# When a cross-attention batch stops counting as open, and the delay of the last two gate tiles

## The chip, the core and the metric

One core of one Trainium2 chip runs the whole program in one launch. The metric is device time in microseconds (us), from the start of an execution to its end. The core has five engines with a queue of their own: PE (TensorE, the matrix products), DVE (VectorE), ACT (ScalarE), POOL (GpSimd) and SP (SyncE, which here issues nearly all transfers). Each engine takes its queue in order, and waits at the head of the queue for what the next instruction needs.

## What is computed

A decoder of two layers over x of 4 batches, 512 rows and 512 columns, each sub-layer followed by a residual sum and a layer norm:

```python
x = ln(x + L0_attn(x))           # A: 4 heads of 128, rotary positions
x = ln(x + gamma*L0_xattn(x))    # B: 8 heads over ctx, softmax over the features
x = ln(x + L0_ffn(x))            # C: quantised gate and up (2048), Hadamard, down
x = ln(x + L1_attn(x))           # D: 16 heads of 32
x = ln(x + L1_xattn(x))          # E: one head over ctx, masked
x = ln(x + L1_ffn(x))            # F: 4-bit weights, 1408 wide, RMS norm

# E, per batch
scores = where(mask, x @ ctx.T / sqrt(512), -1e30)
out = softmax(scores) @ ctx      # zeros if the mask has no True

# C, per batch
h = silu(bitlinear(x, w_gate)) * bitlinear(x, w_up)
y = h_bitlinear(h, w_down)       # Hadamard over 2048, then the product
```

## The kernel before

Every sub-layer works on one batch at a time: 512 rows in four tiles of 128 rows. A unit of work is named by letter and batch, from A0 to F3 (24 of them, `ORDER`, line 38). Each unit is a Python generator. It emits some instructions, yields, and goes on at its next turn. A local `Pipe` (line 43) holds what is to be emitted some turns later: `pipe.later(n, ...)` files it, and each `pipe.tick()` counts one turn down. `pipe.drain()` makes turns with no new work until nothing is left.

**Who runs beside whom** is set by `lanes` (line 1254). One pass of its loop gives each open unit one turn, the older unit first, and then `step` gives one turn to background work. At most two units are open. The next of `ORDER` is opened when fewer than two are open, the same batch of the sub-layer before it is done, and the unit opened last has said "next" (`said >= times`). So a unit's place in the program follows from counting yields. The order of emission sets a priority and is not kept to the letter: the trace shows instructions that come long before their place where their inputs and buffers are free.

**Background work** is listed in `BESIDE` (line 40): a first unit, a last unit, and a key. The key "F" is `l1_ffn_weights`, 33 turns in which the weights of F are brought in: for each of 11 groups two loads of `gu` and one of packed codes `p`, which five turns later are unpacked by DVE and split by ACT and POOL (`p4h`, `p4l`). It gets a turn in each pass while the unit opened last is E2. What is still missing is fetched by `need` inside F0.

**Sub-layer E** (`l1_xattn`, from line 1015), counted in turns from its opening at 0: at 0 the loads of x and of the four ctx_t tiles (`ecT`); at 2 to 5 the four transposes of x (`ex`, split into a high and a low part by ACT and DVE); at 7 the loads of the four ctx tiles (`ecn`), and at 7 to 10 the scores (`es`, twelve products a row tile); "next" at 8; from 10 to 13 minimum and exponent (`ee`, DVE then ACT); at 14 to 17 the transposes `ep`; at 19 to 22 the value products (`pv`, twelve a row tile, in `value_rows`, line 419, which A uses too); at 20 to 23 the residual sums; at 24 the root of the layer norm (`finish`, line 229), at 26 the four norms (line 235, DVE) and at 27 the four stores of x (line 238, SP). At 28 it ends.

**Sub-layer C** (`l0_ffn`, line 607): from turn 9 on, sixteen gate tiles o = 0 to 15, one a turn. Tile o goes through five stages: the products `pg` and `pu` on PE; `gate` (DVE product, ACT Silu), one turn later; `up` (DVE product, ACT copy to `hh`, POOL difference to `hl`), two turns later; `had` (two products on PE), two turns later; `keep` (ACT copy to `hw`), one turn later; and the store to `had_scratch`, two turns later. Then the pipe is drained, sixteen loads bring the scratch back as `z`, two turns pass, and the second Hadamard product (`had2`, line 755) begins.

**Buffers**: pool `o` has 69 tiles of 512 floats a partition (ctx pairs, transposed pairs, F's weights), `t` 13, `x` 12 (three batches), `w` 4 (packed codes before they are split), all on line 27. Eight PSUM banks are shared by all products.

Of the kernel before, what the change touches and what calls it, by code (L numbers as in the profile page):

```python
# [21 lines left out]
B, S, D = 4, 512, 512  # L22
P = 128
NT = 4
# [12 lines left out]
F_SCALED, F_ACT, F_PAIR, F_DOWN = 1, 5, 3, 9  # L37
ORDER = "A0 A1 A2 A3 B0 B1 B2 B3 C0 C1 C2 C3 D0 D1 D2 D3 E0 E1 E2 E3 F0 F1 F2 F3"

BESIDE = [("A1", "A3", "C0"), ("A3", "B0", ("B", 0)), ("B0", "B2", "C"), ("C3", "D0", "D"), ("D1", "D3", "F0"), ("E2", "E2", "F")]  # L40


class Pipe:
# [25 lines left out]
class Net:  # L69
# [349 lines left out]
    def value_rows(self, pipe, pT, v, x, r, phase, b):  # L419

        nc = self.nc
        ln = self.ln_tile()

        def add(ps, i):
            nc.vector.scalar_tensor_tensor(x[i], ps, r[:, i : i + 1], x[i], ALU.mult, ALU.add)
            self.ln_stats(x[i], i, ln)

        for i in range(NT):
            pipe.tick()
            ps = self.pa("pv")  # L430
            self.mm3(ps, [(self.cols(pT[j], slice(i * P, (i + 1) * P)), v[j]) for j in range(NT)])
            pipe.later(1, add, ps, i)
            yield
        yield from pipe.drain()
        self.finish(pipe, x, ln, phase, b)
        yield from pipe.drain()
# [170 lines left out]
    def l0_ffn(self, b):  # L607
        nc = self.nc
        pipe = Pipe()
# [41 lines left out]
            yield  # L651
        scratch = self.had_scratch[b % 2]

        def gate(o, pg, pu):
            g = self.t("g")
            nc.vector.tensor_tensor(g, pg, arow, ALU.mult)
            nc.scalar.activation(g, g, AF.Silu)
            pipe.later(2, up, o, pu, g)

        def up(o, pu, g):  # L660
            nc.vector.tensor_tensor(g, pu, g, ALU.mult)
            hi, lo = self.t("hh", F32R), self.t("hl", F32R)
            nc.scalar.copy(hi, g)  # L663
            nc.gpsimd.tensor_tensor(lo, g, hi.bitcast(F32), ALU.subtract)  # L664
            pipe.later(2, had, o, hi, lo)

        def had(o, hi, lo):
            ph = self.pb("ph")
            nc.tensor.matmul(ph, self.had, hi, start=True, stop=False)
            nc.tensor.matmul(ph, self.had, lo, start=False, stop=True)  # L670
            pipe.later(1, keep, o, ph)

        def keep(o, ph):
            w = self.t("hw")
            nc.scalar.copy(w, ph)

            to = scratch[:, o * P : (o + 1) * P, :].rearrange("i p t -> p i t")
            pipe.later(2, lambda: nc.sync.dma_start(to, w.rearrange("p (i t) -> p i t", i=NT)))

        tern = self.tern  # L680
        for o in range(16):
            pipe.tick()
            c, m = o // 4, slice((o % 4) * P, (o % 4) * P + P)
            self.need("C", lambda: (3, c) in tern["wu_t"])
            pg, pu = self.pa("pg"), self.pa("pu")
            for k in range(NT):
                nc.tensor.matmul(pg, tern["wg_t"][k, c][:, m], qT[k], start=k == 0, stop=k == NT - 1)  # L687
            for k in range(NT):
                nc.tensor.matmul(pu, tern["wu_t"][k, c][:, m], qT[k], start=k == 0, stop=k == NT - 1)  # L689
            pipe.later(1, gate, o, pg, pu)  # L690
            yield "next" if o == 6 else None
# [562 lines left out]
def lanes(order, task, step):  # L1254

    todo = [(e.strip("+!"), e[0] == "+", max(1, e.count("!"))) for e in order]
    plain = [name for name, _, _ in todo]
    live, done = {}, set()  # L1260
    n, said = 0, 9
    while todo or live:
        if todo and len(live) < 2:
            name, soon, times = todo[0]
            before = chr(ord(name[0]) - 1) + name[1]
            if (before in done or before not in plain) and (said >= times or not live or soon):
                todo.pop(0)
                live[name] = task(name)
                last = name
                n, said = n + 1, 0  # L1270
        for name, g in list(live.items()):
            word = next(g, "end")
            if word == "end":
                live.pop(name)
                done.add(name)
            elif word == "next" and name == last:
                said += 1
        step(n)


def body(tc, args, phases=range(6)):
    with ExitStack() as ctx:
        net = Net(ctx, tc, args)
        net.gamma = net.load(net.c("gamma", [P, 1]), args["gamma"].to_broadcast([P, 1]))
        if 0 in phases:
            net.l0_attn_weights()
        net.bg = {("B", 0): net.l0_xattn_ctx(0), "C0": net.l0_ffn_scales(), "C": net.l0_ffn_weights(), "D": net.l1_attn_weights(), "F0": net.l1_ffn_codes(), "F": net.l1_ffn_weights()}
        f = [net.l0_attn, net.l0_xattn, net.l0_ffn, net.l1_attn, net.l1_xattn, net.l1_ffn]
        plain = ORDER.replace("+", "").replace("!", "").split()
        order = ORDER.split() if len(phases) == 6 else ["ABCDEF"[p] + str(b) for p in phases for b in range(B)]  # L1290

        def step(n):
            if len(phases) == 6:
                for first, last, key in BESIDE:
                    if plain.index(first) < n <= plain.index(last) + 1:
                        next(net.bg[key], None)

        def start(name):
            return f["ABCDEF".index(name[0])](int(name[1]))

        lanes(order, start, step)
# [68 lines left out]
```

## Time and profile before

| what | value |
|---|---|
| three runs, median (lowest to highest) | 1580.65 us (1579.52 to 1584.71) |
| the profiled execution's own time | 1581.65 us |
| its span, first to last instruction | 1580.0 us |
| granted TensorE clock, mean | 0.996 |
| PE busy | 1515.4 us, 96% |
| DVE busy | 1232.9 us, 78% |
| ACT busy | 1021.3 us, 65% |
| POOL busy | 666.2 us, 42% |
| C's gate products, first to last start | 461.6 to 691.0 us |
| E's loads of `ecn`, first to last issue | 1139.4 to 1249.9 us |

The profile is of one execution. A busy share is a mean over stages that differ; the time that PE spends idle, 64.6 us in all, is spread over the program in short waits. A row of a timeline gives the start, the duration, engine and line, the operation with the tile that it writes and those that it reads, and in brackets the idle time before it with what ended it. The stretch from about 1165 to 1262 us is E's.

### The profile page before, as it was taken

To read this page: it belongs to the slowest core of one execution; us is meant where nothing else is said; L and a number is where in the kernel's file an instruction comes from. 1 tells how busy PE (TensorE), PEld (TensorE's weight loads), DVE (VectorE), ACT (ScalarE), POOL (GpSimd) and SP (SyncE) were. 2 spreads that over 40 slices of the span, in tenths; PEclk is the share of its full clock that TensorE was granted. 3 is DMA by queue.
4 is the path that set the end of the run, shared out by engine and by line. 5 is a ranking of instruction groups with operands and counts; after the bars stand their busy time and mean duration, and the time that the engine had idled before them with its cause. 6 is when DMAs were issued, how large, how long until landed. Compare 5 with 4: busy or idle time off the path is not lost.

```text
span 1580.0 us, 25595 instructions
## 1 busy us (share of the span) xinstructions
PE 1515.4 (96%) x8222; PEld 1090.1 (69%) x8222; DVE 1232.9 (78%) x2658; ACT 1021.3 (65%) x2208; POOL 666.2 (42%) x672
## 2 busy tenths in 40 slices
PE   8999999999999999899999999999999999999996
PEld 6888786444544674477777668777687777777875
DVE  6486589999976688777577797767786888888896
ACT  5333336988878877888696864969634445545554
POOL 6673663555535303430435323353225344344342
PEclk9999999999999999999999999999999999999998
DMA  7043344455214744653434445633436630020101
GB/s 255 29 157 124 113 154 132 149 173 176 78 48 123 224 137 133 201 185 134 134 102 118 104 141 148 171 97 92 125 123 222 233 110 12 24 81 1 54 1 53
DMA packets 134150, 192.31 MB, mean 122 GB/s; under 512 B 17265, under 2 KB 52081, under 8 KB 134017
## 3 DMA queue, kind: packets, MB, share of 16 engines
q1 hardware_dynamic: 129888, 182.23, 36.3%
q0 software_dynamic: 4128, 8.46, 2.2%
q8 instruction: 65, 1.06, 0.3%
q14 instruction: 69, 0.56, 0.1%
HBM read 117.75 MB, written 47.71 MB: 105 GB/s over the span
## 4 chain that ended last, share of the span: by engine, by line
PE 63%; DVE 17%; ACT 8%; issue 6%; DMA 3%; POOL 3%; SPq 0%; ACTq 0%; DVEq 0%; POOLq 0%
PE fg L1185 7%; PE facc L1168 5%; PE dT L933 3%; DVE fg L1141 3%; PE pg L687 3%; PE had L755 2%; PE dn L741 2%; DVE bsm L474 2%; PE pu L689 2%; ACT de L923 2%; PE bo L498 2%; PE do L953 2%; PE qk L156 2%; PE qk L155 2%; PE qk L154 2%
## 5 line engine op out<-in xcount | busy, mean ns | idle before, releaser
L1141 DVE SCALAR_TENSOR_TENSOR fg<-fg,gs,fg 128x512 f32<-128x512 f32 x220 | 163.2, 745 | 30.9 <-ACT fg L1133 15.3
L923 ACT ACTIVATE de<-de,dm 128x128 f32<-128x128 f32 (+3 forms) x256 | 142.9, 563 | 11.3 <-DVE dm L919 10.9
L1185 PE MATMUL fg<-fxh,gu 128*128 128x512 f32 x352 | 140.2, 398 | 6.1 <-DVE fg L1141 3.1
L919 DVE CUSTOM_DVE_ANT_0 de<-ds,negm,thr 128x128 f32<-128x128 f32 (+3 forms) x256 | 126.4, 546 | 19.4 <-PE ds L908 16.0
L482 POOL TENSOR_SCALAR be<-be,bsm 128x512 f32<-128x512 f32 x128 | 96.5, 766 | 103.8 <-DVE bsm L480 72.7
L1185 PE MATMUL fg<-fxl,gu 128*128 128x512 f32 x352 | 137.4, 390 | 0.1
L664 POOL TENSOR_TENSOR hl<-g,hh 128x512 fp32r<-128x512 f32 x64 | 83.4, 1309 | 110.2 <-ACT hh L663 90.2
L1145 POOL TENSOR_TENSOR fg<-fg,fg 128x512 f32<-128x512 f32 x44 | 60.2, 1367 | 139.6 <-DVE fg L1141 60.0
L476 ACT ACTIVATE be<-bs,bsm 128x512 f32<-128x512 f32 x128 | 87.3, 690 | 31.1 <-DVE bsm L474 29.2
L845 POOL TENSOR_TENSOR dql<-dqf,dqh 128x512 fp32r<-128x512 f32 x32 | 41.4, 1295 | 150.8 <-ACT dqh L844 150.6
L933 PE MATMUL dT<-ident,de 128*128 128x128 f32 x640 | 92.0, 280 | 8.5 <-ACT de L923 6.4
L933 PEld LDWEIGHTS dT<-ident,de 128*128 128x128 f32 x640 | 72.3, 142 | 28.3 <-ACT de L923 14.0
L1185 PEld LDWEIGHTS fg<-fxh,gu 128*128 128x128 f32 x352 | 66.0, 188 | 30.1 <-DVE fg L1141 12.7
L474 DVE TENSOR_REDUCE bsm<-bs 128x1 f32<-128x512 f32 x128 | 83.4, 672 | 0.0
L498 PE MATMUL bo<-bpT,cT 128*64 128x512 f32 x256 | 76.7, 618 | 2.4 <-ACT bpT L489 1.2
L248 PEld LDWEIGHTS bT<-ident,be 128*128 128x128 f32 x512 | 54.9, 141 | 34.0 <-issue 11.5
L248 PE MATMUL bT<-ident,be 128*128 128x128 f32 x512 | 73.2, 281 | 3.6 <-POOL be L482 2.1
L1185 PEld LDWEIGHTS fg<-fxl,gu 128*128 128x128 f32 x352 | 66.1, 188 | 12.8 <-DVE fxl L146 0.4
L352 POOL TENSOR_TENSOR z<-z,rope_cos 128x512 f32<-128x512 f32 x32 | 46.8, 1473 | 64.8 <-DVE zs L349 57.8
L1133 ACT ACTIVATE fg<-fg,gs 128x512 f32<-128x512 f32 x88 | 60.1, 684 | 20.6 <-PE fg L1185 20.4
L687 PE MATMUL pg<-qT,tb 128*128 128x512 bf16 x256 | 66.8, 381 | 4.5 <-ACT qT L649 2.8
L1159 POOL TENSOR_TENSOR fhl<-fg,fhh 128x512 fp32r<-128x512 f32 x44 | 58.5, 1331 | 29.5 <-ACT fhh L1158 29.3
(355 smaller groups left out, 4640.3 us busy)
## 6 DMA issues: line engine op xcount, KB each, us to landing
x<-x SPq DMA_DIRECT2D x176, 256.0 KB, 3.0
had_scratch<-hw SPq DMA_DIRECT2D x64, 256.0 KB, 2.3
z<-had_scratch SPq DMA_DIRECT2D x64, 256.0 KB, 5.8
stk<-dqh SPq DMA_DIRECT2D x192, 64.0 KB, 2.1
tw<-in_wg_t SPq DMA_DIRECT2D x32, 256.0 KB, 3.8
tw<-in_wu_t SPq DMA_DIRECT2D x32, 256.0 KB, 3.7
tw<-in_wd_t SPq DMA_DIRECT2D x32, 256.0 KB, 2.8
p<-in_gu_p SPq DMA_DIRECT2D x22, 256.0 KB, 3.1
```

Source lines behind the costliest of these rows:

```text
L248: self.nc.tensor.transpose(pt[:, i * P : (i + 1) * P], srcs[i][:, j * P : (j + 1) * P], self.ident)
L474: nc.vector.tensor_reduce(sm[:, h : h + 1], ps, AX.X, ALU.max, negate=True)
L476: nc.scalar.activation(e, ps, AF.Exp, bias=sm[:, h : h + 1], accum_out=sm[:, 2 + h : 3 + h])
L482: nc.gpsimd.tensor_scalar(es[h][i], es[h][i], sm[:, 4 + h : 5 + h], 1.0, ALU.mult, ALU.mult)
L498: nc.tensor.matmul(po[0][h * 64 : h * 64 + 64, :], cT[j][:, c : c + 64], pTs[h], start=j == 0, stop=j == NT - 1)
L664: nc.gpsimd.tensor_tensor(lo, g, hi.bitcast(F32), ALU.subtract)
L687: nc.tensor.matmul(pg, tern["wg_t"][k, c][:, m], qT[k], start=k == 0, stop=k == NT - 1)
L919: nc.vector.tensor_tensor_reduce(es[i], ps, self.negm[:, 384 - P * i :], -1.0, self.thr[:, i : i + 1], ALU.add, ALU.min, n4[:, i : i + 1])
L923: nc.scalar.activation(es[i], es[i], AF.Exp, bias=n4[:, i : i + 1], scale=-1.0, accum_out=den[:, hh * 4 + i : hh * 4 + i + 1])
L933: nc.tensor.transpose(pt[:, o + (i - j) * P : o + (i - j + 1) * P], es[i][:, j * P : (j + 1) * P], self.ident)
L1141: self.emitted["DVE"] = nc.vector.scalar_tensor_tensor(y[u], ps, s, y[u], ALU.mult, ALU.add)
L1185: nc.tensor.matmul(ps, self.gu[i, u][:, g * P : (g + 1) * P], xT[g][n], start=n == 0, stop=n == 1)
```

## The change

Four edits. `value_rows` yields "tail" in place of nothing at its first value product if it runs for E. `lanes` notes such units and leaves them out when it counts how many are open; they still get their turns. The window of background work "F" begins with E1 in place of E2. And in C the delays between `gate` and `up`, `up` and `had`, `keep` and the store are one turn for the tiles 14 and 15 and two for the others.

```diff
-BESIDE = [..., ("D1", "D3", "F0"), ("E2", "E2", "F")]
+BESIDE = [..., ("D1", "D3", "F0"), ("E1", "E2", "F")]
...
             pipe.later(1, add, ps, i)
-            yield
+            yield "tail" if phase == 4 and i == 0 else None
...
+        lag = lambda o: 2 if o < 14 else 1
+
         def gate(o, pg, pu):
...
-            pipe.later(2, up, o, pu, g)
+            pipe.later(lag(o), up, o, pu, g)
...
-            pipe.later(2, had, o, hi, lo)
+            pipe.later(lag(o), had, o, hi, lo)
...
-            pipe.later(2, lambda: nc.sync.dma_start(to, w.rearrange("p (i t) -> p i t", i=NT)))
+            pipe.later(lag(o), lambda: nc.sync.dma_start(to, w.rearrange("p (i t) -> p i t", i=NT)))
...
-    live, done = {}, set()
+    live, done, tails = {}, set(), set()
...
-        if todo and len(live) < 2:
+        if todo and len(live.keys() - tails) < 2:
...
             elif word == "next" and name == last:
                 said += 1
+            elif word == "tail":
+                tails.add(name)
```

More of the change, by code (lines that the diff above doesn't have):

```diff
@@ L38 @@
 ORDER = "A0 A1 A2 A3 B0 B1 B2 B3 C0 C1 C2 C3 D0 D1 D2 D3 E0 E1 E2 E3 F0 F1 F2 F3"
-BESIDE = [("A1", "A3", "C0"), ("A3", "B0", ("B", 0)), ("B0", "B2", "C"), ("C3", "D0", "D"), ("D1", "D3", "F0"), ("E2", "E2", "F")]
+BESIDE = [("A1", "A3", "C0"), ("A3", "B0", ("B", 0)), ("B0", "B2", "C"), ("C3", "D0", "D"), ("D1", "D3", "F0"), ("E1", "E2", "F")]
 class Pipe:
```

## The prediction

> **What bounds the kernel now.** I read the page first.
>
> ```profile
> span 1580.0 us, 25595 instructions
> ## 1 busy us (share of the span) xinstructions
> PE 1515.4 (96%) x8222; PEld 1090.1 (69%) x8222; DVE 1232.9 (78%) x2658; ACT 1021.3 (65%) x2208; POOL 666.2 (42%) x672
> ```
>
> PE is busy in all but 1580.0 − 1515.4 = 64.6 us. The change takes no instruction away and adds none; it moves the places of instructions in the queues. So it can win only idle time of PE, and only in C and E and where they hand over. I therefore asked the table of windows for the stretches of E in which PE isn't full (first column the stretch, second its length, third PE's busy time).
>
> ```profile
> 1195.00:1200.00 5.00, 3.22 (x24) 2.27 (x22) 0.00 (x0) 4.85 (x11) 3.39 (x3) 1.00 0.98 332
> 1200.00:1205.00 5.00, 3.94 (x18) 2.82 (x19) 3.94 (x9) 4.67 (x11) 4.10 (x4) 1.00 1.05 397
> 1225.00:1230.00 5.00, 4.74 (x26) 3.40 (x24) 4.97 (x11) 3.42 (x8) 1.76 (x2) 1.00 0.17 49
> 1240.00:1245.00 5.00, 4.41 (x18) 3.04 (x18) 4.22 (x11) 3.27 (x9) 2.81 (x4) 1.00 0.89 329
> 1250.00:1255.00 5.00, 3.94 (x28) 3.26 (x27) 1.72 (x6) 2.17 (x6) 1.27 (x1) 1.00 0.89 291
> 1255.00:1260.00 5.00, 3.96 (x20) 2.16 (x19) 2.73 (x7) 3.94 (x10) 0.00 (x0) 1.00 0.91 291
> ```
>
> Three holes: (a) 1195 to 1205, 1.78 + 1.06 = 2.84 us, where E1 hands over to E2; (b) 0.26 + 0.59 = 0.85 us before and in E3's first scores; (c) 1250 to 1260, 1.06 + 1.04 = 2.10 us, where E3's scores are done and F0 begins. Together 5.79 us; the rest of 1165 to 1262 has next to none. Then the waits of ACT and of SP in E say why (total, times, longest).
>
> ```profile
> ACT ecnh L143 <- DMA ecn<-in_ctx: 15.9, 4, 8.0
> SPq L238 <- DVE x L235: 54.9, 9, 25.8
> SPq L252 <- POOL p4l L146: 19.5, 4, 8.8
> ```
>
> ACT's queue holds the copies `ecnh` ahead of the exponents `ee`. The copies wait for `ecn`. Those loads stand on SP behind the stores of the batch before, and the stores wait for the norms. Last, the timeline of DVE, POOL and PE around (c).
>
> ```profile
> 1189.31 1.92 DVE L235 TENSOR_SCALAR x<-x,ln 128x512 f32<-128x512 f32 x4
> 1244.64 4.85 DVE L235 TENSOR_SCALAR x<-x,ln 128x512 f32<-128x512 f32 x4
> 1244.79 4.42 POOL L146 TENSOR_TENSOR ecnl<-ecn,ecnh 128x512 fp32r<-128x512 f32 x3 [2.17 <-DMA ecn<-in_ctx]
> 1254.21 0.33 PE L248 MATMUL ep<-ident,ee 128*128 128x128 f32 x1 [1.06 <-ACT ee L1042]
> 1256.82 0.50 PE L1185 MATMUL fg<-fxh,gu 128*128 128x512 f32 x1 [0.65 <-DVE fxl L146]
> ```
>
> Four norms take 1.92 us, or 4.85 us when POOL's differences run beside them.
>
> **The "tail" edit.** I counted the yields of every unit. Before, E1 opens 22 passes after E0, E2 9 after E1, E3 20 after E2, F0 9 after E3. After it, 20, 9, 11 and 9. E1 to E2 stays at 9, since there it is "next" (turn 8) that decides. So E shrinks by 11 passes, but a pass has no length of its own; what counts is which PE work lies beside which wait.
>
> Hole (c): before, E3's drain has only F0's four transposes beside it. After, E2's value products stand at E3's turns 8 to 11: tiles 0 and 1 between E3's scores, tile 2 with the last of these, tile 3 behind it. 48 value products ran from 1170.67 to 1181.68, so a row tile costs 11.0/4 = 2.75 us. Tile 3 alone covers more than the 2.10 us. E1's stores also get ready long before E3's scores end, because these are spread over 8 × 2.75 = 22 us in place of 11. What is late next is `fxl`: E2's four sums, statistics and aggregates (0.74 + 0.69 + 0.17 = 1.60 each, 6.4 us) and norms stand among them on DVE. I take 2.0 of 2.1; ends 0 and 2.1.
>
> Hole (b): E3's transposes come when E2 is in its drain and E1 still has value products, so its first scores don't follow bare on E2's last product. I take 0.85; ends 0 and 0.85.
>
> Hole (a): E1 and E2 stand to each other as before, so nothing new covers the wait for the last exponent. Only E1's loads come two passes earlier against E0's stores. Of E1's four `ecn` loads two went at 1180.63, two after the stores at 1191.76. If all go first, ACT is free when the scores end; the chain minimum 0.68, exponent 0.72 + 0.18 remains, about 1.6 us behind the last product, E2's transposes cover part of it, and the second half, E2's split, shrinks likewise. I take half, 1.4; ends −2.9 and +2.8 (the lower end is that hole once more). E in sum: 2.0 + 0.85 + 1.4 = 4.25 us.
>
> **The window edit.** Its passes are 20 before (E2 open to E3 open) and 20 after (9 + 11), so as much of F's weights is brought in: fourteen `gu` and six `p` loads, five groups unpacked. Each unpack costs DVE about 1.7 us (0.54 + 0.48 + 0.68), ACT 0.62, POOL 1.29. All lie beside PE work. What moves are the places on SP: the loads now stand among E1's, not E2's, and a `p` load waits for `p4l` to free a buffer of pool `w`, up to 8.8 us. I cost it at nothing, because in (a) it is E0's stores that come last; uncovered it is the second rival.
>
> **The delay edit.** Per batch the drain loses two turns (tile 13 is now last: 8 turns after the last product become 6), so C2 opens 2 passes earlier and D0 4. From `had` of the last tile to `had2` there are six turns before and after, so the wait for `z` (1.33 us at 557.71, 0.40 at 709.40) stays. PE in the passes of the four drains: full in 500 to 520, 538 to 553 and 682 to 698; 16.32 of 18 us in 646 to 664. Only there is something to win, since `had2` of C2 joins C3's gate products two passes sooner. I take 0.7 of 1.7. On the other side, the chain gate to `had` takes 0.68 + 0.63 + 0.69 + 0.62 + 1.28 = 3.9 us, and PE's cover falls from five passes to three, 2.2 us each where gate products run alone: 6.6 us. Three POOL differences (3.8 us) now meet in two passes. If the cover fails, PE waits one such difference a batch: 4 × 1.28 = 5.1 us. Ends −5.1 and +1.7.
>
> **Sum.** 4.25 + 0.7 = 4.95 us off the profiled execution's 1581.65 (1580.0 of span, 1.65 around it): 1576.7. That execution lies 1.0 us above the median of the runs, 1580.65, so the forecast for the median is 1575.7.
>
> **A rule against it.** The norm rows above show 2.93 us more beside POOL. The Trainium skill, "SBUF — State Buffer", section "Who interferes with whom", says that VectorE in a two-port mode and GpSimd exclude each other from a shared pair of ports, and that the later one blocks fully. Three open batches mean more such meetings: by the rule each of E0 to E2 would pay up to that row's 2.93 us. By it the sum would lose up to 8.8 us if stores were still ahead of the loads that matter; by the row it loses nothing in (c), where the stores now come early.
>
> **The rivals.**
> 1. Order by readiness: the queues follow inputs and buffers more than passes. For it: E3's x was loaded at 1193, when E3 opens near 1233; F's first codes were unpacked by DVE at 1158.9, 40 us ahead of their place. Against it: PE's products keep the order of the passes through all of E. Then about a fifth of the gain comes, 1579.7.
> 2. Slower, by buffers and SP. At E2's last scores the count of `o` tiles by place is 25 for E2 (ctx pairs 8, x pairs 8, second ctx pairs 8, one `ee`), 16 for E1, 24 for F's weights (14 + 10): 65 of 69. Before it was 25 + 16 + 12 = 53. So loads can run ahead less, and the `p` waits come in front of E1's or E2's ctx loads. Price: the longest wait, 8.8 us, in front of `ecn` of E1, whose last pair went only 2.7 us ahead of the end of its scores; the 1.4 us of (a) is lost too. 1575.7 + 1.4 + 8.8 = 1585.9. It decides once such waits pass 4.95 + 4.7 = 9.7 us against the forecast. Against it: DMA is idle in 1185 to 1190 (share 0.04).
> 3. The shortened delay leaves PE waiting for `hl`: 1575.7 + 0.7 + 5.1 = 1581.5. Against it: ACT, not POOL, is nearly full there.
> 4. Much more: every hole of E closes (5.8), C's passes give 1.7, and the start of F0, where PE idles 3.0 us in 1280 to 1325 behind DVE, gains by work done earlier: 10.5 to 12 us, 1569 to 1570.
>
> **Numbers.** 0.3%, 4.7 us, is about what a measurement of this kernel can tell from no change. The bounds are 1575.9 and 1585.4. Forecast 0.52, its own range 1572 to 1577.5 (faster 0.45, same 0.07); rival 1 0.12 (same); rival 2 0.24 (slower 0.21, same 0.03); rival 3 0.06 (same); rival 4 0.06 (faster). Faster 0.51, same 0.28, slower 0.21. The range takes in all but the outer parts of 2 and 4: 1569 to 1587.
>
> **What would show it.** Right: PE full in the last scores of E3, with `pv` among them; all four `ecn` of E1 ahead of E0's stores; `z` waits as before; PE idle lower by some 5 us, all of it in E. Wrong: SP waiting for `p4l` in front of ctx loads; PE waiting for `hl` near `had`; new holes in D or F. The forecast falls if the holes only move to F0's start, where DVE is full.

## The result, and the profile after

The changed kernel takes 1589.97 us (median of 6 runs, 1587.99 to 1591.86); the kernel before took 1583.15 us beside it (1579.52 to 1584.71). The ratio is 1.0043, 95% interval 1.0032 to 1.0055: slower by some 6.8 us. The forecast was 1575.7 us, and the time lies above its range (1569 to 1587). The profiled execution that is read below took 1590.53 us, 1588.7 of it span.

The page of the changed kernel, its head (busy time of each engine, with its share of the span):

```profile
span 1588.7 us, 25593 instructions
PE 1516.9 (95%) x8222; PEld 1093.2 (69%) x8222; DVE 1229.9 (77%) x2658; ACT 1020.0 (64%) x2208; POOL 664.7 (42%) x672
```

The work is the same. TensorE's idle time went from 64.6 us to 1588.7 − 1516.9 = 71.8 us. To see where, I cut both profiled executions at the first matmul of C (`pg`), D (`dx`), E (`ex`) and F (`fg`):

| us | A and B | C | D | E | F |
|---|---|---|---|---|---|
| before | 461.6 | 284.3 | 395.3 | 115.6 | 323.2 |
| after | 462.1 | 288.4 | 395.0 | 118.9 | 324.3 |
| TensorE idle, before | 14.6 | 10.1 | 14.5 | 6.9 | 18.4 |
| TensorE idle, after | 15.4 | 12.9 | 14.6 | 9.5 | 19.4 |

The lengths are differences of starts rounded to a tenth. Each profile is of one execution, and a stage that an edit leaves alone varies as well: in the six profiles, here and below, with the old C and the old buffers, C takes 283.6 to 284.5 us; in the six with the old E and F, E takes 115.6 to 116.5 and F 323.1 to 324.0; A and B together, which no edit touches, take 460.0 to 463.9. So a microsecond in C, E or F says little, three or four do.

C got longer by 4.1 us and E by 3.3 us. E should have become shorter by 4.25. The windows of E around its largest hole (stretch, length, busy time of TensorE, its weight loads, VectorE, ScalarE, POOL, then the granted clock, DMA share and GB/s):

```profile
1195.00:1200.00 5.00, 5.00 (x29) 4.25 (x28) 0.00 (x0) 1.24 (x2) 1.54 (x2) 1.00 1.00 333
1200.00:1207.00 7.00, 0.61 (x6) 0.37 (x4) 4.96 (x8) 2.17 (x5) 4.31 (x4) 0.80 1.05 390
1207.00:1212.00 5.00, 4.39 (x17) 3.59 (x18) 3.33 (x7) 4.67 (x12) 3.98 (x4) 0.50 0.56 206
1212.00:1218.00 6.00, 4.90 (x21) 3.75 (x20) 5.93 (x10) 4.31 (x9) 4.20 (x3) 0.80 0.33 96
1218.00:1222.00 4.00, 4.00 (x19) 3.34 (x18) 2.05 (x4) 1.28 (x3) 0.66 (x1) 1.00 0.96 314
```

At 1200, hole (a)'s place in the order of work (E1's scores done, E2 next), TensorE stands still for 6.39 us (its row is below), and its granted clock is then 0.50 from 1207 to 1212. VectorE did nothing at all from 1195 to 1200. So the question is what VectorE stood before. Its timeline (start, duration, instruction, and in brackets how long it sat idle before it and what released it):

```profile
1192.66 1.92 DVE L235 TENSOR_SCALAR x<-x,ln 128x512 f32<-128x512 f32 x4
1201.97 1.22 DVE L1076 TENSOR_SCALAR p<-p,i 128x512 int32<-128x512 int32 x1 [7.38 <-DMA p<-in_dn_p]
1203.23 1.37 DVE L1077 TENSOR_SCALAR p<-p,i 128x512 int32<-128x512 int32 x1
1204.63 0.69 DVE L1103 SCALAR_TENSOR_TENSOR p<-p,p4s 128x512 f32<-128x512 f32 x1
1205.24 0.68 DVE L1043 CUSTOM_DVE_ANT_0 ee<-es,pen 128x512 f32<-128x512 f32 x1
```

After E0's norms the next entry of its queue is the unpacking of one of F's code groups (lines 1076, 1077, 1103), and that waits 7.38 us for its load. E1's minima (line 1043), for which ScalarE, TensorE and all of E wait, are queued behind it. TensorE's timeline shows the other end:

```profile
1206.83 0.47 PE L248 MATMUL ep<-ident,ee 128*128 128x128 f32 x1 [6.39 <-ACT ee L1044]
1215.58 0.49 PE L156 MATMUL es<-ecTh,exl 128*128 128x512 f32 x1 [1.10 <-DVE exl L146]
1269.17 0.50 PE L156 MATMUL pv<-ecnh,epl 128*128 128x512 f32 x1 [1.50 <-DVE epl L146]
```

The view names ScalarE's exponent as releaser, because that is the last link: minimum, exponent, transpose. The links before it tell the reason. ScalarE's timeline shows how much of the hole is the unpack's:

```profile
1198.50 1.28 ACT L143 CAST ecnh<-ecn 128x512 fp32r<-128x512 f32 x2 [4.30 <-DMA ecn<-in_ctx]
1200.14 0.62 ACT L143 CAST ecnh<-ecn 128x512 fp32r<-128x512 f32 x1 [0.37 <-DMA ecn<-in_ctx]
1200.67 0.61 ACT L143 CAST p4h<-p 128x512 fp32r<-128x512 f32 x1
1205.96 0.72 ACT L1044 ACTIVATE ee<-ee,em 128x512 f32<-128x512 f32 x1 [4.68 <-DVE em L1043]
```

Its copies of `ecn` wait for the context loads, as they did before the change, and end with one `p4h` at 1201.28. Only then does it wait for the minimum, for 4.68 us. So 4.68 of the 6.39 us are the unpack's. By these rows the other 1.7 us, an estimate, would be there without it, since the exponent is queued behind the copies.

And why was the code load late? The timelines of SP's queue and of POOL:

```profile
1193.24 1.78 SPq L238 DMA_DIRECT2D x<-x  x4
1195.08 1.78 SPq L252 DMA_DIRECT2D ecn<-in_ctx  x3
1197.43 0.38 SPq L252 DMA_DIRECT2D p<-in_dn_p  x1
```
```profile
1191.12 1.29 POOL L146 TENSOR_TENSOR p4l<-p,p4h 128x512 fp32r<-128x512 f32 x1 [0.67 <-ACT p4h L143]
```

The load goes out at 1197.43, behind E0's four stores, which wait for the norms, and three `ecn` loads. A `p4l`, which frees a buffer of pool `w`, had ended at 1192.41; the 5 us after that are SP's queue, and the 4.5 us from the issue to 1201.97 are the load itself. In the kernel before a like wait stood in another place: 2.77 us at 1209.84, under E2's scores, where TensorE had work.

```profile
1209.84 1.36 DVE L1074 TENSOR_SCALAR p<-p,i 128x512 int32<-128x512 int32 x1 [2.77 <-DMA p<-in_dn_p]
```

In C the largest new lines of TensorE's waits (total, times, longest) are, after:

```profile
PE ph L672 <- POOL hl L666: 3.1, 4, 1.0
PE had L757 <- DMA z<-had_scratch: 2.2, 2, 1.1
```

Before, the list of C's waits has none for `hl`, and that for `z` came to 1.7 us.

### The profile page after: what moved, and what is told of

Same layout as the page of the kernel before. It is cut to its first block, busy times and chain, and to the rows that moved or that the text cites. A ratio compares the mean times of both kernels' runs of the same rounds, so it can differ in the third digit from the quotient of the medians.

```text
span 1588.7 us, 25593 instructions
## 1 busy us (share of the span) xinstructions
PE 1516.9 (95%) x8222; PEld 1093.2 (69%) x8222; DVE 1229.9 (77%) x2658; ACT 1020.0 (64%) x2208; POOL 664.7 (42%) x672
## 4 chain that ended last, share of the span: by engine, by line
PE 61%; DVE 16%; ACT 9%; issue 6%; DMA 4%; POOL 3%; SPq 0%; ACTq 0%; DVEq 0%; POOLq 0%
PE fg L1187 7%; PE facc L1170 5%; PE dT L935 3%; DVE fg L1143 3%; PE dn L743 2%; PE bo L498 2%; PE pg L689 2%; PE do L955 2%; ACT de L925 2%; PE pu L691 2%; DVE bsm L474 2%; PE bT L248 2%; PE qk L156 2%; PE qk L155 2%; PE qk L154 2%
```

## The experiments

Theory W: the window edit makes E longer, since a code group's unpacking stands in VectorE's queue ahead of E1's minima and waits for its load. Rival R: E waits for the context loads, as rival 2 had it, and the code loads only stand beside that. For C: theory H (TensorE waits for `hl`) and theory O (the older batch's products now displace those of the younger). "Theory A" in the texts recorded ahead of the runs is theory W where a run is about E, and theory H where it is about `hl`.

### The parts by themselves

Four kernels on one chip. The first is the kernel before with the three `lag` lines alone; the second has the "tail" alone; the third has both "tail" and window, with `lag = lambda o: 2`; the fourth has the window alone:

```diff
-("E2", "E2", "F")]
+("E1", "E2", "F")]
```

> The kernel before with the delay edit alone. Theory A (two separate costs: in C the tensor engine waits for hl, in E the vector engine waits for packed codes): slower by 3 to 5 us, since D's first transposes start at 745.9 us before and 750.5 after the change; the waits of PE for hl at ph add up to about 3 us, against 0.3 before. Theory B (all of it comes from three open batches in E): within 1 us of before, and D starts at 746.

> The kernel before with the tail edit alone, background window still E2. Theory A: the unpacking of F's codes no longer stands ahead of E1's minima, so the hole of 6.4 us is gone and the gain forecast for E shows: faster by 2 to 5 us, unless F0 then misses weights (the window has 11 passes in place of 20), which would cost some of it. Theory B: three open batches crowd the buffers and SP: slower by 3 us or more, with holes before E2 and E3.

> Tail and window edits without the delay edit. Theory A: the 6.4 us hole before E1's ep transposes is there, some of the gain at E3 and F0 too: slower by 2 to 4 us, and together with the delay edit alone this sums to the whole change (6.8 us). Theory B: slower by all of 6.8 us.

> The kernel before with the window edit alone: two open batches as before, F's weights from E1 on. Theory A: E1's drain meets the unpacking as in the changed kernel (the same passes after E1 opens), so a hole of about 6 us before E1's ep transposes and no gain at E3: slower by 3 to 6 us. Theory B: no third batch, so within 1 us of before.

The median of before on that chip was 1580.54.

| kernel | median | ratio [95%] | C | E | F |
|---|---|---|---|---|---|
| delay alone | 1583.04 | 1.0017 [1.0009, 1.0026] | 286.9 | 115.6 | 323.1 |
| tail alone | 1579.56 | 0.9996 [0.9987, 1.0005] | 283.8 | 111.4 | 326.6 |
| tail and window | 1585.53 | 1.0032 [1.0020, 1.0045] | 284.5 | 119.1 | 323.7 |
| window alone | 1587.45 | 1.0046 [1.0033, 1.0060] | 283.6 | 123.7 | 320.2 |

Three things follow. The parts add up: 2.5 us for the delay and 5.0 for tail and window make 7.5, where the whole change has 6.8. The window by itself, with two open batches as before, costs 6.9 us: E +8.1, F −3.0. So theory B, that three open batches are the cost, falls. And the tail by itself makes E 4.2 us shorter, but F 3.4 us longer, and the time is the same within what can be told. The delay cost less than expected (2.5 us for 3 to 5), the window more (6.9 for 3 to 6; with the tail 5.0 for 2 to 4).

The 4.2 and 3.4 us are not all idle time. E is cut at F's first `fg`, and with the tail more of E3's products come after that cut: TensorE is busy 1.8 us less in E and 1.0 us more in F. Its idle time falls by 2.5 us in E (6.9 to 4.4) and grows by 2.4 us in F (18.4 to 20.8). TensorE's longest waits around E with the tail alone:

```profile
1195.64 0.33 PE L248 MATMUL ep<-ident,ee 128*128 128x128 f32 x1 [0.95 <-ACT ee L1044]
1199.58 0.50 PE L154 MATMUL es<-ecTh,exh 128*128 128x512 f32 x1 [1.54 <-DVE exl L146]
1255.87 0.50 PE L156 MATMUL pv<-ecnh,epl 128*128 128x512 f32 x1 [1.51 <-DVE epl L146]
```

(b) and (c) are gone, which is the 2.5 us. (a) stays with all its size (0.95 and 1.54 us; the two waits were 1.01 and 1.33 before), and a wait for `epl` is new. What F lost is seen in the windows 1275 to 1325, for the kernel before:

```profile
1275.00:1325.00 50.00, 46.98 (x198) 36.16 (x197) 47.37 (x74) 27.06 (x45) 27.58 (x21) 1.00 0.27 87
```

and for the tail alone:

```profile
1275.00:1325.00 50.00, 45.52 (x186) 33.52 (x186) 48.96 (x71) 25.65 (x43) 30.50 (x22) 1.00 0.36 118
```

With the tail E2 is open 11 passes and not 20 before E3 opens, so with the old window fewer of F's weights are unpacked in E. F0 begins with that work left, on a VectorE that is busy 48.96 of 50 us. That the missing passes are the reason shows in a kernel below that has the tail and 20 passes again: F takes 323.6 us.

### Who stands before the minima

Two kernels, both the changed one with one edit. In the first F's code loads are issued from POOL's queue, past E0's stores; in the second the unpacking comes three turns later, behind E1's minima.

```diff
-            pipe.later(F_LOAD, down, self.load(self.w("p4", I32), a["dn_p"][i]), sc)
+            w = self.w("p4", I32)
+            nc.gpsimd.dma_start(w, a["dn_p"][i])
+            pipe.later(F_LOAD, down, w, sc)
```
```diff
-F_LOAD = 5
+F_LOAD = 8
```

> The changed kernel with the packed-code loads of F's down weights issued from the POOL queue in place of SP's. Theory A (the hole of 6.4 us before E1's ep transposes is VectorE waiting at the head of its queue for a code load that SP issued late, behind E0's stores): the load goes out when its buffer comes free, some 4 to 5 us sooner, the hole shrinks to 1 to 3 us and the kernel is 3 to 5 us faster than the changed one, about 1584 to 1586. Rival R (the ctx loads themselves are late in the crowd of transfers): ACT still waits for ecn, the hole stays above 4 us, the time stays near 1588 to 1590.

> The changed kernel with F_LOAD 8 in place of 5: each unpack stands three turns later behind its load. Theory A: E1's minima come ahead of the unpack on VectorE, the hole shrinks to 1 to 3 us, 3 to 5 us faster than the changed kernel. Rival R: ACT still gets ecn late, hole above 4 us, no gain.

Before took 1582.10 on that chip. Loads on POOL: 1599.66, 1.0112 [1.0095, 1.0129], E 123.2. Later unpacking: 1589.53, 1.0045 [1.0031, 1.0060], E 117.7. So neither mends E, and neither is the 3 to 5 us faster than the changed kernel that was expected. VectorE's timeline with the loads on POOL says why:

```profile
1195.40 0.55 DVE L1076 TENSOR_SCALAR p<-p,i 128x512 int32<-128x512 int32 x1 [0.82 <-DMA p<-in_dn_p]
1210.47 0.55 DVE L1076 TENSOR_SCALAR p<-p,i 128x512 int32<-128x512 int32 x1 [11.44 <-DMA p<-in_dn_p]
1212.18 0.68 DVE L146 TENSOR_TENSOR exl<-ex,exh 128x512 fp32r<-128x512 f32 x1
```

and TensorE's in that kernel:

```profile
1202.67 0.33 PE L248 MATMUL ep<-ident,ee 128*128 128x128 f32 x1 [3.19 <-ACT ee L1044]
1212.92 0.79 PE L154 MATMUL es<-ecTh,exh 128*128 128x512 f32 x1 [6.47 <-DVE exl L146]
```

The first wait fell from 7.38 to 0.82 us and the hole before `ep` from 6.39 to 3.19: the late code load made that part of it. What is left is rival R's. The minima were done at 1199.03, but ScalarE's copies of `ecn` were still held up by the context loads, and the exponent came right behind them without a wait of its own:

```profile
1198.69 0.62 ACT L143 CAST ecnh<-ecn 128x512 fp32r<-128x512 f32 x1 [6.37 <-DMA ecn<-in_ctx]
1201.80 0.72 ACT L1044 ACTIVATE ee<-ee,em 128x512 f32<-128x512 f32 x1
```

The next group's unpacking then waits 11.44 us, and `exl`, E2's split, is queued behind it; TensorE's hole of 6.47 us is now before E2's scores. With the later unpacking the same: the hole before `ep` is 1.46 us, that before `es` 4.63, behind a wait of 10.96. In both the hole follows the entry that stands behind the waiting unpack, from the minima to the splits. Rival R explains what is left before `ep`, but not that. And E gets no shorter than 117.7 by either edit: when the first wait is mended, a second of the same kind is the next to hold E.

### Another window

Two kernels with "tail", old delays, and the window moved: E2 to E3 in the first (20 passes again), E1 alone in the second (9 passes).

```diff
-("E1", "E2", "F")]
+("E2", "E3", "F")]
```
```diff
-("E1", "E2", "F")]
+("E1", "E1", "F")]
```

> The kernel before with the tail edit and the background window from E2 to E3, which again has 20 passes (9 after the tail + 11) but begins, as before, when E2 opens; no delay edit. Theory A: no unpack in front of E1's minima, so E keeps the 4.2 us that the tail alone won there, and F0 doesn't miss weights as it did with the tail alone (F 3.4 us longer): 3 to 5 us faster than before, 1575 to 1578. If three open batches crowd SP and the buffers whatever the window: within 1 us of the tail alone, 1579 to 1580.

> Tail edit with a background window of E1 alone: 9 passes, three code groups, all of them loaded long before E; no delay edit. Theory A: no code load is waited for while E1 is in its drain, so no hole above 2 us before ep; E 110 to 113 us, F longer by 3 to 4 us, since the unpacking is left to F: about 1580. Rival (any unpacking in E1's drain makes the hole): hole above 4 us.

E2 to E3: 1581.02 against 1582.10, 0.9990 [0.9980, 1.0000]; E 114.2, F 323.6. E1 alone: 1587.80 against 1579.78, 1.0048 [1.0035, 1.0061]; E 117.7, F 327.2. VectorE's longest wait for a code load in 1165 to 1290 is 2.4 us in the first and 10.6 in the second. TensorE's hole before E2's scores is 1.25 us in the first and 5.42 in the second, and the half clock is in the second alone (granted clock 1.00 and 0.89 in 1195 to 1225). The rows of E2 to E3, then those of E1 alone:

```profile
1202.16 0.51 PE L154 MATMUL es<-ecTh,exh 128*128 128x512 f32 x1 [1.25 <-DVE exl L146]
1210.83 1.38 DVE L1076 TENSOR_SCALAR p<-p,i 128x512 int32<-128x512 int32 x1 [2.42 <-DMA p<-in_dn_p]
```
```profile
1204.05 1.26 DVE L1076 TENSOR_SCALAR p<-p,i 128x512 int32<-128x512 int32 x1 [10.56 <-DMA p<-in_dn_p]
1205.24 0.68 DVE L146 TENSOR_TENSOR exl<-ex,exh 128x512 fp32r<-128x512 f32 x1
1205.97 0.80 PE L154 MATMUL es<-ecTh,exh 128*128 128x512 f32 x1 [5.42 <-DVE exl L146]
```

So it isn't the length of the window, and not three open batches, which both kernels have. It is that code groups are due while E1 is open. With the window E2 to E3 tail and window cost nothing: E is 1.4 us shorter than before, F 0.4 longer, and the median 1.1 us lower, at the edge of what can be told from no change.

Both forecasts of theory A missed all the same. The first kernel was to be 3 to 5 us faster, and E kept 1.4 of the tail's 4.2 us. In the second all code loads were to be done long before E, with E at 110 to 113 us; one was issued at 1198.62, and the unpack that waited for it stood in front of E2's splits. Before `ep` the hole is 1.59 us there, as forecast.

### Buffers for the code loads

Two kernels with old delays: six buffers, taken from pool T; then five, with the loads on POOL.

```diff
-O_BUFS, T_BUFS, X_BUFS, W_BUFS = 69, 13, 12, 4
+O_BUFS, T_BUFS, X_BUFS, W_BUFS = 69, 11, 12, 6
```
```diff
-O_BUFS, T_BUFS, X_BUFS, W_BUFS = 69, 13, 12, 4
+O_BUFS, T_BUFS, X_BUFS, W_BUFS = 69, 12, 12, 5
...
+            nc.gpsimd.dma_start(w, a["dn_p"][i])
```

> Tail and window edits as in the change, no delay edit, and pool w with 6 buffers in place of 4 (two fewer of pool t, 11 in place of 13, to make room). Theory A (VectorE waits for the code groups five and six, whose loads must wait until the split of an earlier group frees a buffer): all six groups of the window are loaded long before E, the wait of VectorE for codes and the hole of 6.7 us go, E takes 110 to 114 us from its first ex to F's first fg in place of 119.1, 4 to 6 us less than tail and window, some 1580 (the two fewer t buffers may give part of it back in C). Rival (the unpack work itself is too much there, not its wait): E stays above 116.

> The changed kernel with the old delay everywhere, F's integer code loads issued from POOL's queue in place of SP's, and five buffers in place of four for them (one buffer fewer in pool T, which may lengthen C; so E and F are read by themselves). Theory W (VectorE stands before E1's minima and E2's splits because the next code load comes late, and it comes late for want of a buffer and for its place on SP): the longest wait of VectorE for a code load in E falls from 7.4 us (and 11.4 us with the loads on POOL and four buffers) to under 4 us, no hole above 3 us in TensorE's E, and E falls from 118.9 (123.2 with four) to 112 to 116; E and F together 438 to 440. Rival B (the wait is TensorE's and ScalarE's for the context loads, and the code loads only stand beside it): VectorE's waits get shorter, but E stays at 118 us or above.

Six: 1600.66, 1.0134 [1.0121, 1.0148]. C grew by 14 us, as pool T lost two, so the total says nothing on E. In E VectorE's longest wait for a code load fell to 2.5 us and the hole before `ep` to 2.48; E still took 118.9, where theory A had 110 to 114. ScalarE, TensorE and VectorE show what holds it:

```profile
1213.61 1.26 ACT L143 CAST ecnh<-ecn 128x512 fp32r<-128x512 f32 x2 [5.30 <-DMA ecn<-in_ctx]
1217.68 0.33 PE L248 MATMUL ep<-ident,ee 128*128 128x128 f32 x1 [2.48 <-ACT ee L1044]
1220.92 0.69 DVE L146 TENSOR_TENSOR exl<-ex,exh 128x512 fp32r<-128x512 f32 x1 [8.67 <-ACT exh L143]
```

ScalarE stands at its copies of `ecn`, and E1's exponents and E2's splits are queued behind them. So with the code loads early it is rival R, the late context loads, that holds E. The rival in the recorded text, too much unpacking, had E above 116, but not this path.

Five, with the loads on POOL: 1598.47 against 1580.91, 1.0114 [1.0098, 1.0129], E 122.9, and the wait is 12.17 us. Here theory W's expectation failed: a fifth buffer frees nothing, since the load is released by the group before it, whose `p4l` is queued on POOL behind `ecnl` (and that `ecnl` waited 5.17 us for ScalarE's `ecnh`, which waited 6.11 us for `ecn`):

```profile
1207.53 1.26 POOL L146 TENSOR_TENSOR p4l<-p,p4h 128x512 fp32r<-128x512 f32 x1
1209.09 0.56 POOL L1115 DMA_DIRECT2D p<-in_dn_p  x1 [0.30 <-POOL p4l L146]
```

So it is shown that late code loads hold VectorE, and that this makes 4.68 us of the changed kernel's largest hole. That a better place for the code loads alone would give E its 4 us is not shown; the late context loads hold E next. Before, two of E1's four `ecn` loads went ahead of E0's stores (at 1180.63), in the changed kernel one (at 1188.32). Why only one stays open; no run moved the context loads alone.

### The delay edit

Four kernels without tail and with the old window: the delay edit with `hl` of the last two tiles on VectorE; the store's step alone; the two steps of arithmetic alone; and the opposite, one turn longer.

```diff
-            nc.gpsimd.tensor_tensor(lo, g, hi.bitcast(F32), ALU.subtract)
+            (nc.gpsimd if o < 14 else nc.vector).tensor_tensor(lo, g, hi.bitcast(F32), ALU.subtract)
```
```diff
-            pipe.later(2, lambda: nc.sync.dma_start(to, w.rearrange("p (i t) -> p i t", i=NT)))
+            pipe.later(2 if o < 14 else 1, lambda: nc.sync.dma_start(to, w.rearrange("p (i t) -> p i t", i=NT)))
```
```diff
-            pipe.later(2, up, o, pu, g)
+            pipe.later(lag(o), up, o, pu, g)
...
-            pipe.later(2, had, o, hi, lo)
+            pipe.later(lag(o), had, o, hi, lo)
```
```diff
+        lag = lambda o: 2 if o < 14 else 3
```

> The delay edit alone, with the difference hl of the tiles 14 and 15 made by VectorE in place of GpSimd (about 0.7 us in place of 1.28). Theory A (the delay costs because PE reaches the second had product before hl is there): the four waits of PE for hl vanish, C takes as long as before (284 us from its first pg to D's first transpose, 286.9 with the delay edit), the time is within 1 us of before. Rival (the delay costs because had2 and its copies come two passes sooner into C1's and C3's gate tiles): C stays near 287 and the time 2 to 3 us above before.

> The kernel before with only the third delay shortened (keep to the store, tiles 14 and 15): the drain is one pass shorter, gate to had unchanged. Theory O: half of the order effect without any wait for hl, C1's last pg 0.5 to 1.5 us later, the kernel 0.5 to 1.5 us slower. Theory H: no difference.

> The kernel before with the shorter delay on the two steps of arithmetic alone (gate to up, up to had) for the last two tiles; the store of had's result keeps its two passes. Theory Z (what costs is the cover at a pair's end: TensorE's idle time in 540 to 570 and 690 to 724 us is 1.7 us in the kernel before, 3.3 with the whole delay edit, 4.8 with the store's step alone): the waits for hl stay as with the whole edit, 2.5 us in all, the wait for z falls below 1 us in all, since the store has its pass back, and stage C grows by 1.5 to 2.5 us over 284.3; the median is 1 to 2 us above the kernel before. Rival S (the store's step alone is what costs, the waits for hl are paid anyway as other waits): C within 0.5 us of 284.3 and the median equal to the kernel before. Rival O (the order of the gate products at a pair's start costs): C grows by 2.5 us or more, as with the whole edit, with TensorE's idle time at the pair's ends as before.

> The kernel before with the delay edit turned round: three turns in place of two for the tiles 14 and 15. Theory O (the shorter drain costs since the older batch's second Hadamard work goes ahead of the younger batch's gate products, and the younger batch ends last): C1's last pg comes 1 to 2 us sooner after C's start than 76.2 us, C's end 1 to 2.5 us sooner, the kernel 1 to 2 us faster. Theory H (it costs only since PE waits for hl): no more than 0.5 us either way.

TensorE's idle time is given for the two ends of C's pairs and the start of the second pair together (540 to 570, 636 to 690, 690 to 724 us; length less busy time, from the windows):

| kernel | ratio [95%] | idle there | C |
|---|---|---|---|
| before | 1 | 5.8 | 284.3 |
| delay edit alone | 1.0017 [1.0009, 1.0026] | 8.4 | 286.9 |
| and `hl` on VectorE | 1.0039 [1.0026, 1.0053] | 9.4 | 287.9 |
| store's step alone | 1.0030 [1.0019, 1.0041] | 9.6 | 290.3 |
| arithmetic's steps alone | 1.0018 [1.0009, 1.0027] | 8.0 | 286.7 |
| a turn longer | 1.0008 [1.0000, 1.0017] | 5.4 | 284.1 |

In the five other kernels with the old C and the same buffers the idle time there is 5.9 to 7.1 us and C 283.6 to 284.5. So the first four versions stand clear of it in both, and where C grew, most of it is idle time in these three stretches. The waits for `hl` are real (3.1 us in the changed kernel), but theory H falls: with `hl` on VectorE only 0.3 us of them are left, the time isn't within 1 us of before, as was forecast for it, and other waits stand in their place, 1.47 us for ScalarE's `hh` and this one, 2.50 us where the delay edit alone has 0.79:

```profile
559.73 1.13 PE L757 MATMUL had<-had,z 128*128 128x128 f32 x8 [2.50 <-DMA z<-had_scratch]
```

(That profile took 1586.05 us, 3.4 less than the median of its runs; where the rest of that loss lies is not shown.)

The store's step alone has no wait for `hl` and waits 3.50 and 1.26 us before `had2`. For the 3.50 us the view names ScalarE's `q2f`; but SP issued the first load of `z` only at 555.29, after 3.5 us of waiting for a store, and `had2` starts 3.2 us after that, where the shortest landing time of a `z` load is 3.1 us. So I take it for a wait for `z`. The granted clock is 0.51 just behind it (558.5 to 562) and 0.94 in 540 to 570, which at 30 us is another 1.8 us. Both theories on record for this kernel, no loss and 0.5 to 1.5 us, missed its 5 us.

With the arithmetic's steps alone C grows by 2.4 us, as theory Z has it, and rival S falls; the waits for `hl` are 2.4 us, but those before `had2` are still 2.0, 1.2 of them for `z`, where theory Z has less than 1 us. A turn more takes these waits away and wins nothing that can be measured, as the delays of before were long enough. So the chain gate, `hl`, `had`, store, `z`, `had2` needs its cover: in each of the four versions that take a pass from it, TensorE waits at that link or at the next.

Theory O was not tried by itself. For it, `had2` does come 4.2 us sooner while the younger batch's last gate product comes 2.0 to 3.2 us later with the delay edit alone; against it, a turn more brings the gate products 2.0 to 2.9 us sooner, but C ends the same and the kernel is not the 1 to 2 us faster that theory O has. How much of the cost of the store's step alone is the lower clock stays open.

## Why the prediction was wrong

**The step that failed** is "I cost it at nothing, because in (a) it is E0's stores that come last", with "All lie beside PE work" before it. The sum of the unpacks' durations was right, and is no cost. What counts is the place of an unpack in VectorE's queue and when its input comes. The window moved it from under E2's scores to before E1's minima, and a wait of 7.38 us came with it, 4.68 us of it time in which nothing else kept E1's exponents. The prediction listed what the loads are queued behind on SP; it did not ask what is queued behind the unpack on VectorE.

In medians of one chip, edit upon edit: the tail gave 1.0 us where 4.25 were forecast, the window on top of it cost 6.0 where nothing was, and the delay cost 2.5 where a gain of 0.7 was. The window is the largest of the three misses.

**Tail, holes (b) and (c)**: right. Both close with the tail alone: TensorE's idle time in E fell by 2.5 us, where 2.85 was forecast for the two. (a), from which 1.4 was taken, did not shrink (0.95 and 1.54 us). That E's length fell by 4.2 us, and the forecast was 4.25, is luck: 1.8 us of it are products that now come after F's first `fg`. "What is late next is `fxl`" was wrong; it is `epl`, 1.51 us.

**F0's start**: the prediction's condition, "if the holes only move to F0's start, where DVE is full", is what happened with the tail alone: 2.5 us of idle time left E and 2.4 came back in F. E and F together took 438.8 us before, 438.0 with the tail alone and 437.9 with the window E2 to E3. So no more than 1 us was gained there in any version tried, and no version tried is faster than the kernel before by what can be told from no change.

**Delay**: the +0.7 was of the wrong sign, and rival 3 was right in kind. `had2` came 4 us sooner, as the shorter drain promised, but C got 2.6 us longer. The lower bound, TensorE waiting for `hl` with 5.1 us, named the mechanism; measured were 3.1 us in four waits. That TensorE was full in 538 to 553 before the change was read as cover; after it TensorE waits 0.85 us for `hl` there, at 548.73. "The wait for `z` stays" nearly holds (1.73 before, 2.18 after); but with `hl` on VectorE it is 3.5 us, so it seems to stay only since TensorE is already held by `hl`.

**Rival 2** (slower, 1585.9) had the sign, and its place for the trouble, SP's queue, was right. But SP's waits for `p4l` did not grow: 10.4 us in three in 1130 to 1270, the longest 8.3, against 27.1 in five and 8.8 before. And most of the largest hole lies on another path: 4.68 us in front of the unpack on VectorE. The rest is on the rival's path, in front of `ecn` on ScalarE, and in the kernel with six code buffers it is that path that holds E. The order that would have shown the forecast right, all four `ecn` of E1 ahead of E0's stores, did not come: three went at 1195.08, behind them.

**The rule on the ports** ("SBUF — State Buffer", "Who interferes with whom") would have charged each norm of E0 to E2, at the price the prediction took from its own rows, with up to 2.93 us. They took 1.92, 1.91 and 1.92 us, and the 4.85 of before was gone. The rule was not what made this change slow.

## What to carry to other kernels

An instruction that waits for a load costs what is queued behind it, not what it lasts: before moving background work to an earlier stage, look up which entries of its engine's queue it will stand ahead of, and when its load can be issued at the earliest. When such a wait is mended, look for the next one behind it; here it was ScalarE's, for the context loads. A stage whose holes are closed can give nothing if the next stage begins on an engine that is already full, so sum the idle time of both stages, not the length of one. And a delay in a software pipeline is cover: that an engine is full in those passes before a change does not show that the cover is to spare.

## What the runs showed of the hardware

The hole costs more than its length. After 6.39 us without work TensorE's granted clock was 0.50 from 1207 to 1212 and 0.80 on average from 1212 to 1218, and single score products, which last 0.39 us at 1219, lasted 0.63 to 0.80 at 1211 to 1214. In 1195 to 1225 the clock was 0.77 with the loads on POOL (hole of 6.47 us), 0.83 with the window alone (6.75) and 0.89 with the window E1 alone (5.42), and 1.00 in the three kernels whose longest hole there was 1.54 us or less (before, tail alone, window E2 to E3). In C a wait of 3.50 us was followed by 0.51 for 3.5 us, and one of 2.50 us left the clock at 1.00. The Trainium skill, "TensorE: Matmul & The Clock Gate", "What's actually happening", says that the array falls to half its clock after an idle window of about 3.4 us and returns after a busy one as long. These rows agree with the fall; none of them isolates the return, since TensorE was back at work at 1206.83 and its clock was still 0.50 up to 1212.

One run shows that the longest single hole doesn't settle it. With six code buffers it is 2.48 us in E, but with the gaps that follow TensorE is busy 2.65 of the 6 us from 1215 to 1221, and the clock is 0.50 from 1221 to 1232 (columns as above, the clock third from the right):

```profile
1215.00:1218.00 3.00, 0.52 (x5) 0.32 (x4) 0.00 (x0) 2.00 (x5) 3.00 (x4) 1.00 1.03 363
1218.00:1221.00 3.00, 2.13 (x13) 1.24 (x10) 0.08 (x1) 3.00 (x8) 3.00 (x4) 0.77 1.04 395
1221.00:1224.00 3.00, 2.33 (x8) 1.94 (x9) 1.22 (x3) 2.68 (x7) 3.00 (x3) 0.50 1.05 392
1224.00:1228.00 4.00, 1.95 (x7) 1.23 (x6) 3.28 (x7) 3.50 (x8) 2.81 (x3) 0.50 0.66 222
1228.00:1232.00 4.00, 4.00 (x10) 3.13 (x10) 3.96 (x8) 0.87 (x2) 0.38 (x2) 0.50 0.95 286
```
